# Selective scans in turns: D product to TensorE, positive part and copies to ScalarE, table switches in order

## The chip, the cores and the metric

The kernel runs on one core of one Trainium2 chip. The core has five engines that each work through their own list of instructions in order: TensorE (PE in the profile) multiplies matrices into the accumulators (PSUM), VectorE (DVE) and ScalarE (ACT) work element by element, GpSimd (POOL) does the same more slowly, and SyncE (SP) here only issues DMA transfers. Engines wait for each other by semaphores. The metric is the time of one execution on the device in microseconds (us): median 3931.5, from 3927.8 to 3944.6 over three runs. The execution that was profiled has a span of 3937.4 us.

## The reference

The program is a stack of four layers over an input of 8 images, 128 channels, 16 x 16 pixels: a layer that sums absolute differences to weights, a layer of three selective scans (Mamba) with a small attention, attention with a mixture of experts, and eight Performer layers with a spectral filter. The change touches the scans of the second layer alone. There a sequence of 256 pixels with 256 inner channels is scanned in three orders: forwards (f), backwards (b), and with a stride (s). For each:

```
def mamba_branch(u, cw, cb, xw, dw, db, A_log, D):
    uc = silu(causal_conv1d(u, cw, cb))
    proj = uc @ xw.T                     # dt (8), Bm (16), Cm (16)
    delta = softplus(dt @ dw.T + db)
    return selective_scan(uc, delta, -exp(A_log), Bm, Cm, D)

def selective_scan(u, delta, A, Bm, Cm, D):
    dA = exp(delta[..., None] * A)                       # 16 states
    dBu = (delta * u)[..., None] * Bm[:, :, None, :]
    h = a * h + bu                                       # along the sequence
    y = einsum('lbdn,bln->bld', hs, Cm)                  # sum over the states
    return y + u * D
```

## The kernel before, in words

All data are 32-bit floats. Channels lie on the 128 partitions, in two halves h; the 2048 positions (8 images of 256) are cut into 4 blocks of 512 (two images each). A **unit** is one scan order k and one block t; there are 3 x 4 = 12 units. `_scans` (L429) runs over the units, and for each over its 16 states n (L557 to L585).

One state consists of these instructions, each over both halves (128 x 1024 elements):
- SyncE fetches the rows of B and C for this state, spread over all partitions, from a scratch in DRAM into `bcs` (L560; pool `rows`, four buffers).
- ScalarE forms `da` = exp(delta x A) in two instructions of 128 x 512 (L566), and multiplies the first element of each image by 0, so that images do not run into each other (L569). `da` lies in PSUM, with **two buffers** (`pa`, L442).
- GpSimd forms `dbu` = du x B (L571; two buffers).
- VectorE scans along the sequence, writing the states over `da` (L573), and multiplies by C into `hc` (L577; two buffers). This product is what frees `da` and `bcs`.
- TensorE adds `hc` into the accumulator `acc` by multiplying with the identity (L583, recorded at the helper line L234). `acc` has **one buffer** (`py`, L441), and the sum over 16 states is one accumulation.

When a unit is summed up, `finish` (L533) forms y = uc x D + acc on VectorE, in four pieces of 128 x 256, undoing the scan order in the access patterns (L546). It is called at state 0 of the next unit, behind that state's product.

Beside the states, the next unit is prepared in steps (`prepare`, L471), one step after each state from n = 3 on: GpSimd lays out the input `uo`; TensorE convolves it with diagonal matrices (`taps`, made on GpSimd at L466) into `pc`; ScalarE takes Silu into `uc` (L497); TensorE projects to `pp`, ScalarE copies it to `proj` (L505), and SyncE writes that to DRAM. The softplus follows as max(x, 0) + ln(1 + exp(-|x|)) with a correction of rounding: TensorE forms `pd`; ScalarE |x| (L519); VectorE the positive part into `delta` (L520); ScalarE exp (L521); VectorE r = e + 1 (L523) and the correction e = (r - 1) - e (L524); ScalarE ln r (L525); GpSimd r - e, the sum `delta`, and the product `du` = delta x uc (L527, L528, L531).

Silu needs another function table of ScalarE than exp and ln, and each switch is an instruction of its own.

The order of work: the program text is recorded, and a scheduler then lays down each engine's list by its own estimates of when an instruction is ready. Text order is therefore not the order on an engine. In the order of before, VectorE's list has the scans of two states, then the two products, for 88 pairs of states, and scan and product by turns for 16 states, most of them in the first unit. ScalarE's list also lets exp and Silu change places with each other. Only one kind of instruction is held to the text's order, by `keep_in_program_order` in `ln_exp` (L229), which asks for the table with exp and ln.

Of the kernel before, what the change touches and what calls it, by code (L numbers as in the profile page):

```python
# [10 lines left out]
F32 = mybir.dt.float32  # L11
AF = mybir.ActivationFunctionType
ALU = mybir.AluOpType
# [3 lines left out]
P = 128  # L17
B = 8
L = 256
NT = B * L  # L20
BLK = 512
# [4 lines left out]
NST = 16  # L26
DTR = 8
NPROJ = DTR + 2 * NST
BRANCHES = ("f", "b", "s")
# [148 lines left out]
class Env:  # L178


    def __init__(self, ctx, tc, dram, cols):
        self.tc, self.nc, self.dram = tc, tc.nc, dram
        self.cols = cols
        nc = self.nc
        pool = ctx.enter_context(tc.tile_pool(name="shared", bufs=1))
        self.pool = pool
        self.cst = pool.tile([P, dram["cst"].shape[1]], F32, tag="cst", name="cst")
        self.vecs = pool.tile([P, dram["vecs"].shape[1]], F32, tag="vecs", name="vecs")
        self.rows = pool.tile([P, dram["rows"].shape[1]], F32, tag="rows", name="rows")
        self.mean = pool.tile([P, P], F32, tag="mean", name="mean")  # L190
        self.ones = pool.tile([P, P], F32, tag="ones", name="ones")
        self.eps = pool.tile([P, 1], F32, tag="eps", name="eps")
        nc.gpsimd.memset(self.mean, 1.0 / P)
        nc.gpsimd.memset(self.ones, 1.0)
        nc.gpsimd.memset(self.eps, 1e-5)
        self.X = pool.tile([P, NT], F32, tag="X", name="X")

        self.w = {
            k: pool.tile(list(dram[k].shape), F32, tag="w_" + k, name="w_" + k)
            for k in ("in_proj", "xproj", "dtproj", "out_proj", "qkv", "router", "expert_b", "tok", "enc", "dec")  # L200
        }
# [27 lines left out]
    def ln_exp(self):  # L229

        self.tc.keep_in_program_order(self.nc.scalar.preload_act_table_set("natural_log_exp_and_others"))

    def mm(self, out, lhsT, rhs, start=True, stop=True):
        self.nc.tensor.matmul(out, lhsT=lhsT, rhs=rhs, start=start, stop=stop)  # L234


def bc(ap, axis, n):

    a = ap.unsqueeze(axis)
    shape = list(a.shape)  # L240
    shape[axis] = n
    return a.to_broadcast(shape)
# [30 lines left out]
def blk(i):  # L273
    return slice(i * BLK, (i + 1) * BLK)
# [154 lines left out]
def _scans(E, ctx, xn, y, w_in, w_x, w_dt):  # L429
# [6 lines left out]
    nc, tc = E.nc, E.tc  # L436
    one = ctx.enter_context(tc.tile_pool(name="l1one", bufs=1))
# [6 lines left out]
    ident = E.c("ident")  # L444
# [19 lines left out]
    for k, s in enumerate(BRANCHES):  # L464
        for j in range(8):
            nc.gpsimd.tensor_scalar_mul(taps[:, k, j, :], ident, E.v("cw" + s, j))  # L466

    class Unit:
        pass

    def prepare(U, k, t):  # L471

        s = BRANCHES[k]
        U.k, U.t = k, t

        uo = two.tile([P, 2, 2, L + 3], F32, tag="uo", name="uo")
        nc.gpsimd.memset(uo[:, :, :, 0:3], 0.0)  # L477
        for h in range(2):
            src = u[:, h, blk(t)].rearrange("p (b l) -> p b l", l=L)
            dst = uo[:, h, :, 3:]  # L480
            if s == "f":
                nc.gpsimd.tensor_copy(dst, src)
            elif s == "b":
                nc.gpsimd.tensor_copy(dst, src[:, :, ::-1])
            else:
                for b in range(2):
                    nc.gpsimd.tensor_copy(
                        dst[:, b, :].rearrange("p (i s) -> p i s", s=4),
                        src[:, b, :].rearrange("p (s i) -> p i s", s=4),
                    )  # L490
        yield
        U.uc = uc = two.tile([P, 2, BLK], F32, tag="uc", name="uc")
        for h in range(2):
            pc = ps.tile([P, 2, L], F32, tag="s", name="pc")
            for j in range(4):
                E.mm(pc, taps[:, k, 4 * h + j, :], uo[:, h, :, j : j + L], start=j == 0, stop=j == 3)
            nc.scalar.activation(  # L497
                uc[:, h, :], pc.rearrange("p b l -> p (b l)"), AF.Silu, bias=E.v("cb" + s, h)
            )
        yield  # L500
        proj = two.tile([NPROJ, BLK], F32, tag="proj", name="proj")
        pp = ps.tile([NPROJ, BLK], F32, tag="s", name="pp")
        for h in range(2):
            E.mm(pp, w_x[:, k, h, :], uc[:, h, :], start=h == 0, stop=h == 1)
        nc.scalar.copy(proj, pp)  # L505
        U.bc = scratch.tile([NPROJ, BLK], F32, tag="bc", name="bc")
        nc.sync.dma_start(U.bc, proj)
        yield
        E.ln_exp()


        U.delta = delta = two.tile([P, 2, BLK], F32, tag="delta", name="delta")
        e = one.tile([P, 2, BLK], F32, tag="sp_e", name="sp_e")
        r = one.tile([P, 2, BLK], F32, tag="sp_r", name="sp_r")
        for h in range(2):
            pd = ps.tile([P, BLK], F32, tag="s", name="pd")
            E.mm(pd, w_dt[:, k, h * P : (h + 1) * P], proj[0:DTR, :])
            db = E.v("db" + s, h)
            nc.scalar.activation(e[:, h, :], pd, AF.Abs, bias=db)  # L519
            nc.vector.tensor_scalar(delta[:, h, :], pd, db, 0.0, ALU.add, ALU.max)  # L520
        nc.scalar.activation(e, e, AF.Exp, scale=-1.0)  # L521
        yield
        nc.vector.tensor_scalar_add(r, e, 1.0)  # L523
        nc.vector.scalar_tensor_tensor(e, r, -1.0, e, ALU.add, ALU.subtract)  # L524
        nc.scalar.activation(r, r, AF.Ln)  # L525
        yield
        nc.gpsimd.tensor_sub(r, r, e)  # L527
        nc.gpsimd.tensor_add(delta, delta, r)  # L528
        yield
        U.du = du = two.tile([P, 2, BLK], F32, tag="du", name="du")  # L530
        nc.gpsimd.tensor_mul(du, delta, uc)  # L531

    def finish(U):  # L533

        s = BRANCHES[U.k]
        for h in range(2):
            for b in range(2):
                c = slice(b * L, (b + 1) * L)
                dst = y[U.k][:, h, U.t * BLK + b * L : U.t * BLK + (b + 1) * L]
                a0, a1 = U.uc[:, h, c], U.acc[:, h, c]  # L540
                if s == "b":
                    a0, a1 = a0[:, ::-1], a1[:, ::-1]
                elif s == "s":
                    dst = dst.rearrange("p (s i) -> p s i", s=4)
                    a0, a1 = (v.rearrange("p (i s) -> p s i", s=4) for v in (a0, a1))
                nc.vector.scalar_tensor_tensor(dst, a0, E.v("D" + s, h), a1, ALU.mult, ALU.add)  # L546

    units = [(k, t) for k in range(3) for t in range(NBLK)]
    cur, last = Unit(), None
    for _ in prepare(cur, *units[0]):  # L550
        pass
    for i, _ in enumerate(units):
        nxt, steps = None, iter(())
        if i + 1 < len(units):
            nxt = Unit()
            steps = prepare(nxt, *units[i + 1])
        for n in range(NST):  # L557
            bcs = rows.tile([P, 2, BLK], F32, tag="bcs", name="bcs")
            at = cur.bc[DTR + n : DTR + n + 1, :]
            nc.sync.dma_start(  # L560
                bcs, bass.AP(at.tensor, at.offset, [[0, P], [NST * BLK, 2], [1, BLK]])
            )
            da = pa.tile([P, 2, BLK], F32, tag="da", name="da")
            for h in range(2):
                a = neg_a[:, cur.k, h * NST + n : h * NST + n + 1]
                nc.scalar.activation(da[:, h, :], cur.delta[:, h, :], AF.Exp, scale=a)  # L566

            first = da.rearrange("p h (b l) -> p (h b) l", l=L)[:, :, 0:1]
            nc.scalar.mul(first, first, 0.0)  # L569
            db = two.tile([P, 2, BLK], F32, tag="dbu", name="dbu")  # L570
            nc.gpsimd.tensor_tensor(db, cur.du, bc(bcs[:, 0, :], 1, 2), ALU.mult)  # L571
            flat = da.rearrange("p h l -> p (h l)")
            nc.vector.tensor_tensor_scan(  # L573
                flat, flat, db.rearrange("p h l -> p (h l)"), 0.0, ALU.mult, ALU.add
            )
            hc = two.tile([P, 2, BLK], F32, tag="hc", name="hc")
            nc.vector.tensor_tensor(hc, da, bc(bcs[:, 1, :], 1, 2), ALU.mult)  # L577
            if n == 0:
                if last is not None:
                    finish(last)  # L580
                cur.acc = py.tile([P, 2, BLK], F32, tag="y", name="acc")
            for h in range(2):
                E.mm(cur.acc[:, h, :], ident, hc[:, h, :], start=n == 0, stop=n == NST - 1)  # L583
            if n >= 3:
                next(steps, None)  # L585
        for _ in steps:
            pass
        cur, last = nxt, cur
# [841 lines left out]
```

## Time and profile before

| what | us |
|---|---|
| median time of three runs | 3931.5 |
| span of the profiled execution | 3937.4 |
| first layer, up to the first scan | 1254.6 |
| scans, from the first scan to the last D product | 813.5 |
| attention, fusion and what follows, to 2500 us | 431.9 |
| the rest | 1437.0 |

| in the scan stage | busy us | share of 813.5 |
|---|---|---|
| VectorE | 710.8 | 87% |
| TensorE | 560.7 | 69% |
| GpSimd | 536.8 | 66% |
| ScalarE | 370.4 | 46% |

How to read the profile's lines. A group of instructions has its source line, engine, operation, output and inputs by the program's names, the shapes, and the count; then total busy us and the mean ns of one; then the engine's idle us just ahead of these instructions, and what ended most of it. A line of the timeline has the start in us from the span's start, the us it lasts, engine, line, operation, and the count of like instructions that were merged into it; in brackets the idle time ahead of it and what ended that. "PEclk" is the share of full clock that TensorE was granted, "DMA" the mean busy share of the 16 DMA engines.

### The profile page before, as it was taken

What the parts mean: (1) busy time and instruction counts of PE and PEld (TensorE: products, weight loads), DVE (VectorE), ACT (ScalarE), POOL (GpSimd) and SP (SyncE); (2) the same over time, 40 slices, a digit from 0 to 9 for tenths busy, and PEclk for the clock granted to TensorE, in tenths of its full rate; (3) what the DMA queues carried; (4) which work ended last, traced back from release to release, by engine and by line L of the source; (5) the groups of instructions that cost most, each with busy time, mean ns of one, the idle gap of its engine ahead of it and who ended that gap; (6) DMA issues with size and microseconds to landing.
All of it is one profiled execution on the core that took longest, in us unless ns stands there. A gap on an engine that the chain in (4) does not pass through costs nothing. (4 is left out here: it accounts for less than half of the span.)

```text
span 3937.4 us, 38553 instructions
## 1 busy us (share of the span) xinstructions
PE 3352.6 (85%) x15140; PEld 1684.2 (43%) x15140; DVE 2713.6 (69%) x2920; ACT 2179.7 (55%) x2453; POOL 883.5 (22%) x585
## 2 busy tenths in 40 slices
PE   7999999999998666676768967889999999994999
PEld 3333333333332222222225433366666666662676
DVE  7999999999996988888883123456555555654111
ACT  6999999999995454444531131145554555542111
POOL 0000000000004767666651000122222222220000
PEclk9999999999999889888889986899999999996999
DMA  1000000000001444444430000000000000002000
GB/s 36 1 1 1 1 1 1 1 1 1 1 1 50 129 129 123 124 120 129 119 112 24 0 0 28 30 1 12 12 2 11 12 12 2 11 1 86 0 0 11
DMA packets 62722, 131.59 MB, mean 33 GB/s; under 512 B 4178, under 2 KB 10596, under 8 KB 61772
## 3 DMA queue, kind: packets, MB, share of 16 engines
q1 hardware_dynamic: 60044, 126.01, 10.5%
q10 hardware_dynamic: 2496, 3.11, 0.3%
q8 instruction: 119, 1.95, 0.2%
q14 instruction: 63, 0.52, 0.0%
HBM read 127.08 MB, written 2.03 MB: 33 GB/s over the span
## 5 line engine op out<-in xcount | busy, mean ns | idle before, releaser
L403 ACT ACTIVATE d<-sh,w 128x2048 f32<-128x2048 f32 x576 | 1094.8, 1991 | 80.3 <-PE o L234 70.9
L395 DVE SCALAR_TENSOR_TENSOR acc<-sh,w,acc 128x2048 f32<-128x2048 f32 x448 | 1023.4, 2407 | 0.1
L234 PE MATMUL o<-d,sel 128*32 128x512 f32 x4608 | 928.4, 598 | 12.0 <-ACT d L403 12.0
L234 PE MATMUL acc<-hc,cst 128*128 128x512 f32 x768 | 450.4, 737 | 250.3 <-DVE hc L577 226.5
L234 PEld LDWEIGHTS o<-d,sel 128*32 128x32 f32 x4608 | 322.9, 109 | 563.1 <-issue 412.7
L571 POOL TENSOR_TENSOR dbu<-du,bcs 128x1024 f32<-128x1024 f32 x192 | 449.6, 2357 | 236.2 <-DVE da L573 120.3
L573 DVE TENSOR_TENSOR_SCAN da<-da,dbu 128x1024 f32<-128x1024 f32 x192 | 432.2, 2287 | 91.3 <-ACT da L569 72.9
L566 ACT ACTIVATE da<-delta,neg_a 128x512 f32<-128x512 f32 x384 | 257.3, 687 | 385.9 <-DVE hc L577 381.4
L234 PEld LDWEIGHTS acc<-hc,cst 128*128 128x128 f32 x768 | 169.6, 233 | 527.0 <-DVE hc L577 307.9
L234 PE MATMUL o<-acc,sel 128*32 128x512 f32 x1024 | 292.9, 610 | 45.2 <-DVE acc L395 45.2
L477 POOL MEMSET uo<- 128x12 f32 x12 | 1.3, 112 | 1183.5 <-PE o L234 1169.5
L577 DVE TENSOR_TENSOR hc<-da,bcs 128x1024 f32<-128x1024 f32 x192 | 225.1, 1211 | 1.2
L1375 DVE COPY ug<-p 128x256 f32<-128x256 f32 (+1 forms) x96 | 49.3, 514 | 232.0 <-PE p L234 232.0
L988 DVE SCALAR_TENSOR_TENSOR k<-pq,bias,cst 128x512 f32<-128x512 f32 x64 | 45.1, 747 | 195.6 <-PE pq L234 195.6
L1373 ACT COPY ug<-p 128x256 f32<-128x256 f32 (+1 forms) x96 | 42.6, 444 | 239.2 <-PE p L234 239.2
L234 PE MATMUL p<-T,ut 128*128 128x256 f32 x768 | 172.0, 383 | 0.0
L234 PE MATMUL pq<-u,we 128*128 128x512 f32 x256 | 129.6, 612 | 46.2 <-DVE k L988 46.2
L393 DVE TENSOR_SCALAR acc<-sh,w 128x2048 f32<-128x2048 f32 x128 | 162.7, 1342 | 6.4 <-POOL sh L345 6.4
L234 PEld LDWEIGHTS o<-acc,sel 128*32 128x32 f32 x1024 | 66.2, 111 | 219.1 <-issue 146.9
L234 PEld LDWEIGHTS p<-T,ut 128*128 128x128 f32 x768 | 147.8, 193 | 24.6 <-issue 3.1
L1035 ACT COPY kp<-pf 128x704 f32<-128x704 f32 x64 | 47.8, 746 | 180.1 <-PE pf L234 180.1
L1064 POOL TENSOR_TENSOR kp<-kp,off 128x704 f32<-128x704 f32 x64 | 86.4, 1367 | 209.2 <-DVE off L1050 209.2
(314 smaller groups left out, 4707.4 us busy)
## 6 DMA issues: line engine op xcount, KB each, us to landing
bcs<-bc SPq DMA_DIRECT2D x192, 512.0 KB
m<-in_Mphi SPq DMA_DIRECT2D x4, 2048.0 KB
lw<-in_layers SPq DMA_DIRECT2D x8, 944.0 KB
f<-in_fuse SPq DMA_DIRECT2D x2, 1152.0 KB
T<-in_phi ACTq DMA_DIRECT2D x1, 2048.0 KB
x<-in_x SPq DMA_DIRECT2D x4, 256.0 KB
rows<-in_brow SPq DMA_DIRECT2D x8, 128.0 KB
out_y<-fin SPq DMA_DIRECT2D x4, 256.0 KB
```

Source lines behind the costliest of these rows:

```text
L234: self.nc.tensor.matmul(out, lhsT=lhsT, rhs=rhs, start=start, stop=stop)
L393: nc.vector.tensor_scalar(acc, tap(0), w[:, 0, f : f + 1], None, ALU.max)
L395: nc.vector.scalar_tensor_tensor(acc, tap(k), w[:, k, f : f + 1], acc, ALU.max, ALU.add)
L403: nc.scalar.activation(d, tap(k), AF.Abs, scale=-1.0, bias=w[:, k, f : f + 1])
L566: nc.scalar.activation(da[:, h, :], cur.delta[:, h, :], AF.Exp, scale=a)
L571: nc.gpsimd.tensor_tensor(db, cur.du, bc(bcs[:, 0, :], 1, 2), ALU.mult)
L573: nc.vector.tensor_tensor_scan(flat, flat, db.rearrange("p h l -> p (h l)"), 0.0, ALU.mult, ALU.add)
L577: nc.vector.tensor_tensor(hc, da, bc(bcs[:, 1, :], 1, 2), ALU.mult)
L988: nc.vector.scalar_tensor_tensor(x, pq[:, r, :].rearrange("p (b l) -> p b l", l=L), w["bias"][:, b : b + 1], bc(E.c(table), 1, 2), ALU.add ...
L1035: nc.scalar.copy(kp[:, 2 * b : 2 * b + 2, :], pf[:, :, 0:HM])
L1064: nc.gpsimd.tensor_tensor(kp[:, cs, :].rearrange("p c (h m) -> p c h m", m=M), kp[:, cs, :].rearrange("p c (h m) -> p c h m", m=M), bc(off ...
L1375: nc.vector.tensor_copy(dst, p4)
```

## The change

Four things are done, all inside the scans:
- **Turns.** A new helper, `after(key, ins)`, ties an instruction behind the last one with the same key in the scheduler's graph, without a semaphore. With the key "scan" VectorE's list is held to scan, product, scan, product.
- **Tables.** With the key "tables" the Silu, the explicit switch back to the table of exp and ln, and all Exp and Ln of the scans keep the text's order on ScalarE, so that there is one switch each way per unit.
- **D on TensorE.** Diagonal matrices of D (`dd`) are made once on GpSimd. `acc` starts with dd x uc, and the states are added to it; so `finish` only has to copy `acc` out, which ScalarE does in two pieces of 128 x 512.
- **Softplus.** The positive part becomes a Relu with bias on ScalarE, and r = e + 1 an Identity with bias there. The correction e stays on VectorE.

VectorE is left with scan, product and one correction per unit.

```
+    def after(self, key, ins):
+        last = self.chains.get(key)
+        if last is not None:
+            self.tc.add_manual_dep(
+                ins.ins,
+                last.ins.name,
+                mybir.DependencyInfo(mybir.DependencyClass.NoSync, mybir.DependencyReason.DATA),
+                reason=key,
+            )
+        self.chains[key] = ins
...
+    dd = one.tile([P, 6, P], F32, tag="dd", name="dd")
+    for k, s in enumerate(BRANCHES):
+        for h in range(2):
+            nc.gpsimd.tensor_scalar_mul(dd[:, 2 * k + h, :], ident, E.v("D" + s, h))
...
-            nc.scalar.activation(
-                uc[:, h, :], pc.rearrange("p b l -> p (b l)"), AF.Silu, bias=E.v("cb" + s, h)
+            E.after(
+                "tables",
+                nc.scalar.activation(uc[:, h, :], pc.rearrange("p b l -> p (b l)"), AF.Silu, bias=E.v("cb" + s, h)),
             )
+        E.after("tables", nc.scalar.preload_act_table_set("natural_log_exp_and_others"))
...
-        E.ln_exp()
...
-            nc.vector.tensor_scalar(delta[:, h, :], pd, db, 0.0, ALU.add, ALU.max)
-        nc.scalar.activation(e, e, AF.Exp, scale=-1.0)
+            nc.scalar.activation(delta[:, h, :], pd, AF.Relu, bias=db)
+        E.after("tables", nc.scalar.activation(e, e, AF.Exp, scale=-1.0))
         yield
-        nc.vector.tensor_scalar_add(r, e, 1.0)
+        nc.scalar.activation(r, e, AF.Identity, bias=E.ones[:, 0:1])
         nc.vector.scalar_tensor_tensor(e, r, -1.0, e, ALU.add, ALU.subtract)
-        nc.scalar.activation(r, r, AF.Ln)
+        E.after("tables", nc.scalar.activation(r, r, AF.Ln))
...
-            for b in range(2):
-                c = slice(b * L, (b + 1) * L)
-                dst = y[U.k][:, h, U.t * BLK + b * L : U.t * BLK + (b + 1) * L]
-                a0, a1 = U.uc[:, h, c], U.acc[:, h, c]
...
-                nc.vector.scalar_tensor_tensor(dst, a0, E.v("D" + s, h), a1, ALU.mult, ALU.add)
+            dst = y[U.k][:, h, blk(U.t)].rearrange("p (b l) -> p b l", l=L)
+            a = U.acc[:, h, :].rearrange("p (b l) -> p b l", l=L)
...
+            nc.scalar.copy(dst, a)
...
-                nc.scalar.activation(da[:, h, :], cur.delta[:, h, :], AF.Exp, scale=a)
+                E.after("tables", nc.scalar.activation(da[:, h, :], cur.delta[:, h, :], AF.Exp, scale=a))
...
-            nc.vector.tensor_tensor_scan(
-                flat, flat, db.rearrange("p h l -> p (h l)"), 0.0, ALU.mult, ALU.add
+            E.after(
+                "scan",
+                nc.vector.tensor_tensor_scan(
+                    flat, flat, db.rearrange("p h l -> p (h l)"), 0.0, ALU.mult, ALU.add
+                ),
             )
-            nc.vector.tensor_tensor(hc, da, bc(bcs[:, 1, :], 1, 2), ALU.mult)
+            E.after("scan", nc.vector.tensor_tensor(hc, da, bc(bcs[:, 1, :], 1, 2), ALU.mult))
...
             for h in range(2):
-                E.mm(cur.acc[:, h, :], ident, hc[:, h, :], start=n == 0, stop=n == NST - 1)
+                if n == 0:
+                    E.mm(cur.acc[:, h, :], dd[:, 2 * cur.k + h, :], cur.uc[:, h, :], start=True, stop=False)
+                E.mm(cur.acc[:, h, :], ident, hc[:, h, :], start=False, stop=n == NST - 1)
```

More of the change, by code (lines that the diff above doesn't have):

```diff
@@ L183, in __init__ @@
         self.cols = cols
+        self.chains = {}
         nc = self.nc
@@ L536, in finish @@
         for h in range(2):
-            for b in range(2):
-                c = slice(b * L, (b + 1) * L)
-                dst = y[U.k][:, h, U.t * BLK + b * L : U.t * BLK + (b + 1) * L]
-                a0, a1 = U.uc[:, h, c], U.acc[:, h, c]
[L541 to L546, printed above, removed]
+            dst = y[U.k][:, h, blk(U.t)].rearrange("p (b l) -> p b l", l=L)
+            a = U.acc[:, h, :].rearrange("p (b l) -> p b l", l=L)
+            if s == "b":
+                a = a[:, :, ::-1]
+            elif s == "s":
+                dst = dst.rearrange("p b (s i) -> p b s i", s=4)
+                a = a.rearrange("p b (i s) -> p b s i", s=4)
+            nc.scalar.copy(dst, a)
     units = [(k, t) for k in range(3) for t in range(NBLK)]
```

## The prediction

> **What bounds the kernel now.** I read the page's busy shares first, then the busy time of the scan stage as one stretch, then the groups, and last the order of time on each engine. The change touches only the scans, which run from the first scan at 1254.6 us to the last D product at 2068.1 us:
>
> ```profile
> core 0: us, PE busy (x) PEld busy (x) DVE busy (x) ACT busy (x) POOL busy (x), PEclk, DMA share, GB/s
> 1254.62:2068.09 813.47, 560.73 (x1014) 211.38 (x1012) 710.76 (x476) 370.36 (x677) 536.81 (x259) 0.85 0.42 123
> ```
>
> VectorE (DVE) is busy 711 of 813 us (87%), TensorE 69%, GpSimd (POOL) 66%, ScalarE (ACT) 46%, the DMA engines 42%. So VectorE bounds the stage, yet 103 us of it are idle. The page's groups say what a state costs:
>
> ```profile
> L571 POOL TENSOR_TENSOR dbu<-du,bcs 128x1024 f32<-128x1024 f32 x192 | 449.6, 2357 | 236.2 <-DVE da L573 120.3
> L573 DVE TENSOR_TENSOR_SCAN da<-da,dbu 128x1024 f32<-128x1024 f32 x192 | 432.2, 2287 | 91.3 <-ACT da L569 72.9
> L566 ACT ACTIVATE da<-delta,neg_a 128x512 f32<-128x512 f32 x384 | 257.3, 687 | 385.9 <-DVE hc L577 381.4
> L577 DVE TENSOR_TENSOR hc<-da,bcs 128x1024 f32<-128x1024 f32 x192 | 225.1, 1211 | 1.2
> ```
>
> Nearly all of VectorE's idle time here is ahead of the scan, 72.9 us of it for `da`, while ScalarE itself idles 381 us waiting for the product `hc` (L577), which frees `da`. Each waits for the other over two buffers. The timeline of VectorE shows why. In the first unit states stand in turns, scan, product, scan, product:
>
> ```profile
> 1292.05 2.30 DVE L573 TENSOR_TENSOR_SCAN da<-da,dbu 128x1024 f32<-128x1024 f32 x1 [2.23 <-POOL dbu L571]
> 1294.44 1.23 DVE L577 TENSOR_TENSOR hc<-da,bcs 128x1024 f32<-128x1024 f32 x1
> 1295.59 2.29 DVE L573 TENSOR_TENSOR_SCAN da<-da,dbu 128x1024 f32<-128x1024 f32 x1
> 1297.96 1.23 DVE L577 TENSOR_TENSOR hc<-da,bcs 128x1024 f32<-128x1024 f32 x1
> 1299.11 2.29 DVE L573 TENSOR_TENSOR_SCAN da<-da,dbu 128x1024 f32<-128x1024 f32 x1
> ```
>
> A state takes 1299.11 - 1295.59 = 3.52 us with no gap. In later units two scans stand ahead of two products:
>
> ```profile
> 1371.59 4.48 DVE L573 TENSOR_TENSOR_SCAN da<-da,dbu 128x1024 f32<-128x1024 f32 x2 [1.08 <-ACT da L569]
> 1375.98 2.33 DVE L577 TENSOR_TENSOR hc<-da,bcs 128x1024 f32<-128x1024 f32 x2
> 1379.40 4.48 DVE L573 TENSOR_TENSOR_SCAN da<-da,dbu 128x1024 f32<-128x1024 f32 x2 [1.08 <-ACT da L569]
> 1383.79 2.33 DVE L577 TENSOR_TENSOR hc<-da,bcs 128x1024 f32<-128x1024 f32 x2
> 1388.52 1.66 DVE L546 SCALAR_TENSOR_TENSOR yf<-uc,vecs,acc 128x256 f32<-128x256 f32 x4 [2.40 <-PE acc L234]
> 1390.09 4.47 DVE L573 TENSOR_TENSOR_SCAN da<-da,dbu 128x1024 f32<-128x1024 f32 x2
> ```
>
> Here no `da` is free until the first product of a pair, so the scan waits 1.08 us in each: 1379.40 - 1371.59 = 7.81 us for two states, against 7.04 in turns. The last lines show the end of a unit: VectorE waits 2.40 us for TensorE's last sum and spends 1.66 us on the D product (L546). In the instruction order of before, 88 pairs hold 176 of the 192 states; 16 stand alone.
>
> **What the Trainium skill says.** "ScalarE: Activation LUTs", What ACT_TABLE_LOAD costs, puts a switch of tables at 1283 ns for the load and some 1380 ns more for a drain. The trace agrees on the load (1283 ns) and not on the drain: an activation starts 1.30 us after the load that began at 1321.97. I use 1.28. "SBUF — State Buffer", Who interferes with whom, says that a VectorE instruction with two SBUF inputs, or in a two-port mode, and a GpSimd instruction reading SBUF block each other whole. The trace agrees: the `r` addition (L523) took 0.68 us once and 2.06 us beside `dbu`. That addition leaves VectorE; the subtraction behind it (L524, two SBUF inputs) stays. "Perfetto Trace Analysis", Optimizing Scalar/DVE Operations, allows moving work from a saturated VectorE to ScalarE; at 46% busy ScalarE has room on average, so order within a unit decides.
>
> **The change, part by part.**
>
> *Turns.* 88 pairs x (7.81 - 7.04) = 68 us gone, if nothing else ends the wait. In turns ScalarE has this much room:
>
> ```profile
> 1302.74 1.42 ACT L566 ACTIVATE da<-delta,neg_a 128x512 f32<-128x512 f32 x2 [1.92 <-DVE hc L577]
> 1304.19 0.16 ACT L569 ACTIVATE da<-da 128x4 f32<-128x4 f32 x1
> ```
>
> So `da` is ready 1.72 us after its buffer comes free, and wanted 3.52 us after: 1.8 us of slack per state.
>
> *Off VectorE.* Per unit the D product (1.65 to 2.4 us, plus up to 2.75 of waiting), the positive part (1.40) and the addition (0.7 to 2.1) leave; about 6 us x 11 or 12.
>
> *Onto ScalarE.* Per unit two Relu of 128x512 from PSUM (0.69 each, as Abs at L519), one Identity of 128x1024 (1.06, as L521), two copies of 128x512. Copies from strided PSUM are not in the trace: at least 0.69; at most 1.4 times that (L546 rises from 476 to 655 ns in the strided branch), 0.95. I take 0.8. Table loads fall from 38 to about 26 of 1.28 us.
>
> *Onto TensorE.* 24 products (two 0.5 us passes each), about 2 us a unit beside 48.8 of 68.7 busy: hidden under VectorE. They queue behind the two copies, since `acc` has one buffer: last product of the unit, 2.1 us; copies, to 3.7; four matmuls, to 7.6. The third product of the new unit needs its `hc` back at 9.3 us. It costs nothing.
>
> *New waits.* I follow one unit with these durations, from the end of `hc` of state 2 as time 0, in the instruction order of the changed program:
> - State 4: exponentials to 1.5, load to 2.8, first Silu to 3.5, the small multiplication to 3.7. Its scan was due at 3.52: 0.2 lost. Second Silu and load back run to 5.65.
> - State 5: exponentials to 7.1, the copy of `proj` to 7.6, ready 7.8 where 7.27 was due: 0.6 lost. Product 5 ends at 11.4, product 6 at 14.9.
> - The softplus stands ahead of state 7. TensorE gives `pd` at 10.3 (behind product 4); Abs, Relu, Abs, Relu and Exp end at 14.15; an exponential, then Identity, end at 15.9. VectorE, free at 14.9, holds the subtraction L524 next, with every scan queued behind it: 1.05 lost waiting, 1.2 running. Scan 7 starts at 17.15 rather than 14.9: 2.25.
> - Ln ends at 18.3, state 8 is ready in time at 19.9. GpSimd's order is subtraction, `dbu` 9, addition, product `du`, `dbu` 10, at 2.35 each from 18.3: 30.1. Scan 10 was due at 27.7: 2.4 lost. The first unit of before shows the same sequence and loss (2.23, first line of its timeline above):
>
> ```profile
> 1280.31 2.36 POOL L527 TENSOR_TENSOR sp_r<-sp_r,sp_e 128x1024 f32<-128x1024 f32 x1
> 1282.62 2.35 POOL L571 TENSOR_TENSOR dbu<-du,bcs 128x1024 f32<-128x1024 f32 x1
> 1284.93 2.36 POOL L528 TENSOR_TENSOR delta<-delta,sp_r 128x1024 f32<-128x1024 f32 x1
> 1287.37 2.35 POOL L531 TENSOR_TENSOR du<-delta,uc 128x1024 f32<-128x1024 f32 x1
> 1289.67 7.10 POOL L571 TENSOR_TENSOR dbu<-du,bcs 128x1024 f32<-128x1024 f32 x3
> ```
>
> A unit is then 16 x 3.52 + 0.2 + 0.6 + 2.25 + 2.4 = 61.8 us; the last one, which prepares nothing, 56.3. Before, starts of units lie 67.2, 68.3, 69.3 and 68.7 apart, the last took 62.2.
>
> *Start.* The first unit's softplus has no cover: two Relu, and 1.06 for a 0.69 addition, delay the first scan by some 2.7 us, also counting a 0.6 us copy of `uo` that now precedes `du` on GpSimd. The six diagonal matrices of D (0.6 us each, as `taps`) end before the projections that TensorE must finish first; hidden.
>
> *Sum.* First scan 1257.3, 11 x 61.8 = 680, 56.3, and 4 for the last sum and copies: 1997 against 2068, so 71 us less. The orders before and behind the scans are the same, so I carry their time over: 3931.5 - 71 = 3860.
>
> **The rivals.**
> 1. *The new waits vanish.* If GpSimd and the softplus ran earlier than I follow them, only L524 remains: 57.5 a unit, 47 us more saved, 3813. Against: the loss of 2.23 is already in the trace under this order.
> 2. *New waits replace old ones.* ScalarE keeps a fixed order, so a copy waiting for TensorE, or Relu for `pd`, holds the exponentials; and rows must arrive each 3.52 us rather than 3.9. At 65.5 a unit, 41 of 71 us are lost again: 3901. For: GpSimd waits 114.8 us for `bcs` now. Against: those waits come with pairs, which free rows two at a time; in the first unit's turns GpSimd waits only for scans. A row is asked for at a product's end and its `dbu` falls due 5.8 us later, with 2.4 more to spare; in the pairs a `dbu` that waited for its row began at 1341.2, 4.9 us after the product that freed the row's buffer.
> 3. *Slower.* If ScalarE's held order cost over 6.9 us a unit beyond mine, nothing is left; at 72 a unit, 3972. Against: ScalarE's work per unit is 16 x 1.58 for the states and some 12 for preparation and copies, 37 of 62 us.
>
> **How the numbers follow.** My course 0.78; rival 1 0.07; rival 2 0.12; rival 3 0.03. The predicted time is 3860. The strided copies (0.69 to 0.95) and the collision at L524 (up to 2.35 us more a unit, 26 in all) and a better overlap on GpSimd (2.4 less, 26) span 3834 to 3886; runs of before differ by 17 us; I widen to 3830 to 3892, halfway to either rival. Rival 2 at its worst falls within 0.5% of before, so: faster 0.94, same 0.03, slower 0.03.
>
> **What would show it.** Scans and products strictly in turns, `da` waits ahead of the scan down from 72.9 us to some 20; no `delta` or `y` on VectorE; per unit one wait near 1 us at L524 and one near 2.4 us for `dbu`; units 62 us apart, scan stage near 742 us. I am wrong if a wait for `bcs` or the copies shows ahead of scans in most states, if units lie over 65 us apart, or if a later stage moves by more than 10 us.

## The result and the profile after

| | us |
|---|---|
| before, median of 4 executions beside it | 3934.6 (3927.8 to 3944.6) |
| after, median of 4 executions | 3876.7 (3868.5 to 3889.0) |
| after / before | 0.9853 [0.9819, 0.9888] |
| after measured again, median of 6 | 3870.0 (3862.8 to 3877.4) |
| after again / before beside it | 0.9823 [0.9793, 0.9854] |

The forecast was 3860. The busy time of the scan stage of after, from the first scan to 2002.00 us, half a microsecond before the last copy of the last sum ends (columns as for before):

```profile
core 0: us, PE busy (x) PEld busy (x) DVE busy (x) ACT busy (x) POOL busy (x), PEclk, DMA share, GB/s
1257.59:2002.00 744.41, 534.24 (x1062) 190.64 (x1062) 684.52 (x395) 407.23 (x726) 539.19 (x257) 0.96 0.55 134
```

The stage is 69 us shorter than 813.47. VectorE is busy 684.5 us of 744.4 (92%, 87% before) and has 60 us idle instead of 103. The groups of after's page that answer to those of before:

```profile
L587 POOL TENSOR_TENSOR dbu<-du,bcs 128x1024 f32<-128x1024 f32 x192 | 451.2, 2353 | 171.5 <-DVE da L591 169.7
L591 DVE TENSOR_TENSOR_SCAN da<-da,dbu 128x1024 f32<-128x1024 f32 x192 | 439.7, 2290 | 49.1 <-POOL dbu L587 37.7
L582 ACT ACTIVATE da<-delta,neg_a 128x512 f32<-128x512 f32 x384 | 265.4, 691 | 296.0 <-DVE hc L596 285.1
L596 DVE TENSOR_TENSOR hc<-da,bcs 128x1024 f32<-128x1024 f32 x192 | 235.2, 1225 | 18.3 <-issue 1.3
```

The idle time ahead of the scan fell from 91.3 to 49.1 us, and what ends it has changed: 37.7 us are now for `dbu` from GpSimd; for `da`, which took 72.9 before, the list of waits has 10.4. Of the 37.7, 11.7 are the wait for the very first scan, which lies ahead of the stage; the other 26 are eleven waits of 2.36. The 18.3 us ahead of the product (L596) are 0.1 us between each scan and its own product; they are part of the 3.52 us of a state in turns. The timeline of VectorE shows what stands in the way of a unit of pure turns:

```profile
1276.30 2.30 DVE L591 TENSOR_TENSOR_SCAN da<-da,dbu 128x1024 f32<-128x1024 f32 x1 [0.94 <-ACT da L585]
...
1282.21 1.23 DVE L596 TENSOR_TENSOR hc<-da,bcs 128x1024 f32<-128x1024 f32 x1
1283.57 2.07 DVE L542 SCALAR_TENSOR_TENSOR sp_e<-sp_r,sp_e 128x1024 f32<-128x1024 f32 x1
1285.56 2.28 DVE L591 TENSOR_TENSOR_SCAN da<-da,dbu 128x1024 f32<-128x1024 f32 x1
...
1298.56 2.30 DVE L591 TENSOR_TENSOR_SCAN da<-da,dbu 128x1024 f32<-128x1024 f32 x1 [2.36 <-POOL dbu L587]
```

Three losses stand in each of the eleven units that prepare another, always at the same states: about 1 us where the Silus hold up `da` (state 5), 2.2 us at the correction L542 (ahead of state 7), 2.4 us for `dbu` (state 10). GpSimd's timeline over the same stretch shows where the last two come from:

```profile
1282.20 2.36 POOL L587 TENSOR_TENSOR dbu<-du,bcs 128x1024 f32<-128x1024 f32 x1 [1.16 <-DVE da L591]
1286.81 2.36 POOL L545 TENSOR_TENSOR sp_r<-sp_r,sp_e 128x1024 f32<-128x1024 f32 x1 [2.25 <-ACT sp_r L543]
1289.12 2.36 POOL L587 TENSOR_TENSOR dbu<-du,bcs 128x1024 f32<-128x1024 f32 x1
1291.43 2.36 POOL L546 TENSOR_TENSOR delta<-delta,sp_r 128x1024 f32<-128x1024 f32 x1
1293.87 2.35 POOL L549 TENSOR_TENSOR du<-delta,uc 128x1024 f32<-128x1024 f32 x1
1296.18 4.64 POOL L587 TENSOR_TENSOR dbu<-du,bcs 128x1024 f32<-128x1024 f32 x2
```

Sum and product of the softplus (L546, L549) stand back to back ahead of the `dbu` that the scan of 1298.56 waits for: 1296.18 + 2.35 = 1298.5. And the correction starts at 1283.57 while the `dbu` of 1282.20 runs to 1284.56; it ends 1.08 us after that. Alone it takes 1.21 us, beside `dbu` 2.07. The Trainium skill, "SBUF — State Buffer", Who interferes with whom, says that a VectorE instruction with two SBUF inputs and a GpSimd instruction that reads SBUF shut each other out, whoever issues first going on to its end; these starts and ends agree.

Then the stages. "Scans" ends here with the last product `hc`; "fusion" is the rest of the second layer, its small attention included; "behind" is everything from the start of the third layer to the end, and the expert layer is counted from its first expert product to the weights of the next layer:

| profile | first scan | scans | fusion | behind | of it the expert layer |
|---|---|---|---|---|---|
| before | 1254.6 | 809.0 | 209.0 | 1664.8 | 71.8 |
| after | 1257.6 | 741.7 | 207.7 | 1680.2 | 96.0 |
| after, again | 1256.1 | 741.9 | 206.8 | 1665.6 | 66.7 |

The scans of after repeat within 0.2 us, those of before within 1.3 (experiment 7). The work behind them took 15 us longer in the first profile of after, and no longer in the second, with the same program.

### The profile page after: what moved, and what is told of

It reads as the page before. It is cut to its first block, busy times and chain, and to the rows that moved or that the text cites. A ratio compares the mean times of both kernels' runs of the same rounds, so it can differ in the third digit from the quotient of the medians.

```text
span 3887.2 us, 38606 instructions
## 1 busy us (share of the span) xinstructions
PE 3342.9 (86%) x15188; PEld 1665.6 (43%) x15188; DVE 2685.0 (69%) x2836; ACT 2213.5 (57%) x2500; POOL 890.9 (23%) x591
## 5 line engine op out<-in xcount | busy, mean ns | idle before, releaser
L247 PE MATMUL acc<-hc,cst 128*128 128x512 f32 x768 | 406.1, 653 | 204.1 <-DVE hc L596 204.1
L591 DVE TENSOR_TENSOR_SCAN da<-da,dbu 128x1024 f32<-128x1024 f32 x192 | 439.7, 2290 | 49.1 <-POOL dbu L587 37.7
L582 ACT ACTIVATE da<-delta,neg_a 128x512 f32<-128x512 f32 x384 | 265.4, 691 | 296.0 <-DVE hc L596 285.1
L247 PEld LDWEIGHTS acc<-hc,cst 128*128 128x128 f32 x768 | 139.7, 200 | 462.7 <-DVE hc L596 357.2
L596 DVE TENSOR_TENSOR hc<-da,bcs 128x1024 f32<-128x1024 f32 x192 | 235.2, 1225 | 18.3 <-issue 1.3
```

Of the source, the lines that this page charges most:

```text
L582: E.after("tables", nc.scalar.activation(da[:, h, :], cur.delta[:, h, :], AF.Exp, scale=a))
L591: nc.vector.tensor_tensor_scan(flat, flat, db.rearrange("p h l -> p (h l)"), 0.0, ALU.mult, ALU.add),
L596: E.after("scan", nc.vector.tensor_tensor(hc, da, bc(bcs[:, 1, :], 1, 2), ALU.mult))
```

## The experiments

In what follows "scans" is the stage length of this table. Ratios are to the kernel before, run on the same chip beside each.

**1. The turns alone.** The kernel before, with only this added:

```
+            E.after("scan", nc.vector.tensor_tensor_scan(...))
+            E.after("scan", nc.vector.tensor_tensor(hc, da, bc(bcs[:, 1, :], 1, 2), ALU.mult))
```

> The kernel before, with scan and product tied in turns and nothing else changed. Theory 1 (turns carry about half of the gain, the moved work the other half): VectorE keeps about 6 us of positive part, addition, correction and D product per unit, so a unit takes 16 x 3.52 + 6 + the GpSimd wait of 2.4 = 64 to 66 us against 68.7; the scan stage shrinks by 30 to 55 us from 813, the time is 3880 to 3905. Rival (turns are all of it): the scan stage is as in the changed kernel, 744 us, a gain of some 69. Rival (turns are nothing without the moves, because the waits for the last sum and the ScalarE table switches fill the gaps again): within 15 us of before.

Measured: 3898.2 us, 0.9887 [0.9853, 0.9921]; scans 757.5, which is 51.5 less than before, as theory 1 had it, and 15.8 more than after. VectorE is as busy as before (710.8 against 708.3 us): the whole gain is idle time, 100.7 to 46.7 us. Added first, the order of two kinds of instruction gives three quarters of the change's gain in the stage (51.5 of 67.3). The parts do not simply add up: taken out of the whole change, the same order costs more than the whole gain (experiment 2).

**2. The moves without the turns.** The kernel after, with two scans held ahead of two products in all 96 pairs of states (`product()` holds the product `hc`, `finish` and the sums):

```
+            held.append(product)
+            if n % 2:
+                for go in held:
+                    go()
+                held.clear()
```

> The changed kernel, with all its moves, but VectorE's list tied in pairs, two scans and then two products, through all 96 pairs. Theory 1: each pair waits for a free buffer again, 7.81 us or more against 7.04; a unit takes 62.5 plus 2 for the correction and up to 4 for the table switch, 64.5 to 68 us against 62.2; scan stage 775 to 820 against 744; 30 to 75 us slower than the changed kernel. Rival (the moves alone carry the gain): within 10 us of the changed kernel.

Measured: 3949.6 us, 1.0022 [1.0004, 1.0039]; scans 822.6, 80.9 more than after and more than either theory gave. From the waits of this kernel (total us, times, longest):

```profile
POOL dbu L588 <- DMA bcs<-bc: 191.7, 62, 4.5
DVE da L592 <- ACT da L586: 139.4, 91, 4.2
```

A pair waits 139.4/91 = 1.53 us for `da` on average, not 1.08, and GpSimd's waits for `bcs`, 114.8 us before, have grown to 191.7. VectorE is 48 us less busy than before (660.4 against 708.3, by the profile) and the stage is 14 us longer. Relieving the busiest engine was worth nothing as long as a wait for two buffers set the pace. The 14 us cannot all be laid to the moves: this kernel has 8 pairs more than before, some 6 us by an estimate from the 0.77 us that a pair of before lost against turns, and ScalarE's held order besides.

**3. The D product back on VectorE.** The kernel after, with `finish` and the first sum as before:

```
-            nc.scalar.copy(dst, a)
+                nc.vector.scalar_tensor_tensor(dst, a0, E.v("D" + s, h), a1, ALU.mult, ALU.add)
...
-                    E.mm(cur.acc[:, h, :], dd[:, 2 * cur.k + h, :], cur.uc[:, h, :], start=True, stop=False)
```

> The changed kernel with the D product and the copy out of the accumulator back on VectorE as before (four pieces, behind the first product of the next unit), and no dd product on TensorE. Theory: in turns TensorE has finished by then, so VectorE does not wait, and the move is worth its busy time alone, 1.65 us a unit in orders f and b and 2.4 in s: scan stage 742 + 20 to 25. Rival 1: the wait for the last sum of up to 2.75 us comes back too, + 45. Rival 2: the time falls into waits that are there anyway, under 5.

Measured: 3914.7 us, 0.9935 [0.9914, 0.9957]; scans 760.2, 18.5 more than after, a little under the theory's 20 to 25. VectorE is 19.4 us busier; its waits for `dbu` and `da` are the same 37.7 and 10.4 us. In turns the product has its sum at hand: but for the very last unit (2.1 us) VectorE does not wait for it, where the pairs of before showed 2.40. So this part is worth its busy time on VectorE and nothing else.

**4. Positive part and r = e + 1 back on VectorE.**

```
-            nc.scalar.activation(delta[:, h, :], pd, AF.Relu, bias=db)
+            nc.vector.tensor_scalar(delta[:, h, :], pd, db, 0.0, ALU.add, ALU.max)
...
-        nc.scalar.activation(r, e, AF.Identity, bias=E.ones[:, 0:1])
+        nc.vector.tensor_scalar_add(r, e, 1.0)
```

> The changed kernel with the positive part and r = e + 1 back on VectorE. Theory: VectorE gets 1.4 and 0.7 to 2.1 us a unit more, but the chain on ScalarE ahead of the correction gets 2.4 us shorter, so the wait there goes and the move is worth nothing: scan stage within 10 us of 742. Rival: the busy time comes on top, + 23 to 38.

Measured: 3920.2 us, 0.9946 [0.9930, 0.9963]; scans 775.5, 33.8 more than after: my theory fell. The amount lies in the rival's range, but busy time is only part of it: VectorE is 20.9 us busier (705.4 against 684.5) and idles 12.9 us more. ScalarE's waits in this kernel:

```profile
ACT da L582 <- DVE hc L596: 266.3, 135, 5.5
ACT sp_r L543 <- DVE sp_e L542: 88.0, 11, 8.0
```

The logarithm L543 waits 8.0 us a unit for the correction (15.0 us in all in after, 1.4 a unit). It stands in the held order of ScalarE's tables, so the exponentials behind it wait too; VectorE's wait for `da` rises from 10.4 to 45.3 us, while that for `dbu` falls from 37.7 to 19.4. Experiment 1 lays the wait for `da` to the order held on ScalarE and not to the place of the three instructions. There they are on VectorE too, and the D product besides, but ScalarE's order is free:

```profile
DVE da L588 <- ACT da L582: 9.8, 11, 0.9
ACT sp_r L538 <- DVE sp_e L537: 18.9, 11, 1.7
```

Its stage is 18.0 us shorter than here (757.5), with more work on VectorE. Where the D product stands does not bear on this wait: experiment 3 has 10.4 as after does.

**5. ScalarE's order left to the scheduler.** The key "tables" taken from Silu, Exp and Ln, and `ln_exp` put back:

```
-                E.after("tables", nc.scalar.activation(da[:, h, :], cur.delta[:, h, :], AF.Exp, scale=a))
+                nc.scalar.activation(da[:, h, :], cur.delta[:, h, :], AF.Exp, scale=a)
```

> The changed kernel without the order of tables on ScalarE (the former request for the table of exp and ln in its old place). The built order then has 77 table loads in the scans instead of some 24, about 53 x 1.28 = 68 us more on ScalarE. Theory: many are alone in a state and fit into the 1.8 us of room there, but those next to a Silu or the softplus come on top: scan stage + 10 to 40. Rival: ScalarE has room on average (55% busy), so under 5.

Measured: 3881.6 us, 0.9858 [0.9824, 0.9893]; scans 733.5, 8.2 less than after. The trace shows 71 table loads in the stage instead of 22, some 63 us more on ScalarE at 1.28 each, and they did not lengthen the stage; that theory fell. The scheduler parts the two Silus and puts the correction where GpSimd mostly is not reading (mean 1.40 us, 2.07 in after). VectorE waits 30.0 us for `da` and 27.0 for `dbu`, together no less than in after; it is 9.4 us less busy (675.1 against 684.5), most of it the correction. So the held order of tables, one of the four parts of the change, did not pay in the stage. The time as a whole is not below that of after (0.9858 against 0.9853 and 0.9823); the one profile here has the longer time behind the scans (experiment 7).

**6. The change once more.**

> The changed kernel once more, for a second profile. Theory A (the loss of 27 us in the expert layer, where TensorE ran at half its clock, belongs to that one execution): the scan stage is again 744 us within 2, and the expert layer, from its first bias product to the weights of the next layer, takes near 75 us as before rather than 101. Theory B (the denser scans cause it): the expert layer takes some 100 us again.

Its numbers are in the section on the result. Theory A holds: 741.9 for the scans (744 counts to the last copy), 66.7 instead of 96.0 for the expert layer (72.1 instead of 101.4 if counted from the first bias product, as the expectation does). In the first profile of after, over three stretches of 10 us of that layer:

```profile
2375.00:2385.00 10.00, 10.00 (x12) 3.17 (x11) 2.45 (x4) 0.00 (x0) 0.00 (x0) 0.50 0.00 0
2385.00:2395.00 10.00, 10.00 (x12) 3.02 (x11) 1.68 (x3) 0.00 (x0) 0.00 (x0) 0.50 0.00 0
2395.00:2405.00 10.00, 10.00 (x15) 3.21 (x14) 2.75 (x4) 0.00 (x0) 0.00 (x0) 0.67 0.00 0
```

and the same stretches of the second:

```profile
2375.00:2385.00 10.00, 10.00 (x22) 3.43 (x22) 3.76 (x6) 0.00 (x0) 0.00 (x0) 1.00 0.00 0
2385.00:2395.00 10.00, 10.00 (x23) 3.29 (x21) 3.79 (x6) 0.00 (x0) 0.00 (x0) 1.00 0.00 0
2395.00:2405.00 10.00, 10.00 (x21) 3.71 (x21) 4.12 (x6) 0.00 (x0) 0.00 (x0) 0.92 0.00 0
```

The layer starts at 2369.7 in both. TensorE is busy throughout; in one execution it is granted half its clock (third column from the right) for over 25 us, in the other it has the full clock within 5. In both it had begun to work 9 us before the layer, at half its clock, after the same idle time (6.63 and 6.64 us). So neither the work nor the gap ahead of it tells the two apart.

**7. The kernel before once more**, to see whether it too takes the longer way behind the scans.

> The kernel before once more, with a profile. Theory A (the stages behind the scans take one of two times in any kernel, whatever its scans do): the scan stage takes 809 within 3 us, and the stages from the attention on take either about 1665 us, as in the first profile, or about 1678, as in most profiles of the kernel after. Theory B (the moves of the change made the later stages slower): always about 1665 here. One more profile at 1678 settles it for A; one at 1665 leaves it where it is.

Measured: 3937.5 us, 1.0002 [0.9988, 1.0016]; scans 807.7, behind 1661.5. That leaves the matter where it was for before. Over all fourteen profiles of this study the part behind the scans falls into two groups of seven, 1659 to 1666 us and 1676 to 1682. They are the groups of the expert layer too: 67 to 72 us in the seven short ones, 88 to 96 in the seven long ones. Both profiles of before lie in the lower, but so do the second of after and those of experiments 2, 9 and 10, which contain every move of work of the change (experiment 2 without its turns). So the moves do not force the longer time; whether they make it more frequent is open.

**8. Spreading GpSimd's work, first try.** The kernel after, with the softplus on GpSimd tied between the `dbu` of states 8, 9 and 11, and two more ScalarE instructions held in order:

```
-        nc.scalar.copy(proj, pp)
+        E.after("tables", nc.scalar.copy(proj, pp))
...
+        E.after("pool", nc.gpsimd.tensor_sub(r, r, e))
+        yield
+        E.after("pool", nc.gpsimd.tensor_add(delta, delta, r))
...
+            E.after("pool", nc.gpsimd.tensor_tensor(db, cur.du, bc(bcs[:, 0, :], 1, 2), ALU.mult))
```

> The changed kernel, with GpSimd's three softplus instructions spread over four states and tied in that order among the dbu, and the small multiplication and the copy of proj tied in order on ScalarE, so that the Silu no longer stands between an exponential and its scan. Theory (the waits that I followed in the unit are single, and vanish when their cause is moved): the 2.36 us wait for dbu goes from each of 11 units, 26 us, and of 1.1 us at the Silu some 0.7 remain at most; the scan stage is 705 to 720 against 744. Rival (the waits only move on, since GpSimd's work per unit has to be done somewhere): less than 10 us.

Measured: 3874.2 us, 0.9838 [0.9796, 0.9879]; scans 737.3, 4.4 less than after: a miss, and the rival's case. The wait for `dbu` did fall, 37.7 to 21.6, but that for `da` rose from 10.4 to 23.2: the copy of `proj`, now held in place, waits 3 us a unit for TensorE (32.6 us in all) with the exponentials behind it. The two ties on ScalarE were not tried one by one; experiment 11 has the small multiplication tied and the copy free, and a wait for `da` of 10.2.

**9. Only GpSimd's list ordered.** The ties on ScalarE taken out again, and the layout of `uo` moved two units ahead, behind state 5.

> The changed kernel, where GpSimd's list alone is held to an order: its three softplus instructions at states 8, 9 and 11, and the layout of uo at state 5, for the unit after the next. ScalarE's list is left as in the changed kernel. Theory (each of GpSimd's extra 2.35 us fits into the 1.17 us of idle time of two states, if they do not stand together): the 2.36 us wait for dbu goes from every unit and nothing comes in its place, scan stage 742 - 26 = 716. Rival (as in the first try at this, the wait moves on): 730 or more.

Measured: 3849.4 us, 0.9776 [0.9750, 0.9801]; scans 718.8. On another occasion:

> The kernel with only GpSimd's order changed, once more on this chip for comparison: scan stage 719 within 3 us; the stages behind it either some 1665 or some 1678 us; time 3845 to 3865.

3843.3 us, 0.9755 [0.9732, 0.9778]; scans 718.8, and these waits on VectorE:

```profile
DVE da L600 <- POOL dbu L596: 14.4, 5, 10.8
DVE da L600 <- ACT da L594: 10.4, 11, 0.9
```

Of the 14.4, 10.8 are the first scan. The eleven waits of 2.36 have shrunk to 3.6 us in all, and the stage by 22.9: this loss of after was GpSimd's order.

**10. The softplus in pieces.** Besides, each Silu with its own table switch in states 3 and 4, the softplus one piece per state, and the correction between scan and product:

```
+        E.after("scan", nc.vector.scalar_tensor_tensor(e, r, -1.0, e, ALU.add, ALU.subtract))
+        yield
+        E.after("tables", nc.scalar.activation(r, r, AF.Ln))
+        E.after("pool", nc.gpsimd.tensor_sub(r, r, e))
```

> The spread kernel of before, with one Silu and its own table switch in each of states 3 and 4, the small multiplication tied in ScalarE's order, and the softplus cut into one piece per state, the correction on VectorE between the scan and the product of state 9, so that GpSimd makes no B u beside it. Theory: with no other wait left in a unit the correction costs 1.2 us instead of 2.07 and the wait for da at the Silus goes, so that a unit takes about 57.6 us and the scan stage 690 to 703 us (718.8 before); time about 3825. Rival: the waits move on to operations that ScalarE's held order now puts behind a matmul of TensorE, and the stage stays at 715 or more.

Measured: 3875.6 us, 0.9848 [0.9817, 0.9879]; scans 743.5, 25 more than experiment 9. The correction did take 1.21 us as meant, but VectorE waited 43.8 us for `dbu`. GpSimd's timeline:

```profile
1546.25 2.35 POOL L553 TENSOR_TENSOR sp_r<-sp_r,sp_e 128x1024 f32<-128x1024 f32 x1 [3.37 <-ACT sp_r L552]
1548.55 2.35 POOL L599 TENSOR_TENSOR dbu<-du,bcs 128x1024 f32<-128x1024 f32 x1
1550.86 2.35 POOL L555 TENSOR_TENSOR delta<-delta,sp_r 128x1024 f32<-128x1024 f32 x1
1553.17 2.34 POOL L599 TENSOR_TENSOR dbu<-du,bcs 128x1024 f32<-128x1024 f32 x1
1555.48 2.34 POOL L558 TENSOR_TENSOR du<-delta,uc 128x1024 f32<-128x1024 f32 x1
```

It idles 3.37 us for the logarithm with a `dbu` that could have run behind it, and then has 2.35 + 2.35 = 4.7 us of work in each of three states, where a state lasts 3.52.

**11. The same pieces, two states apart.** The Silus in states 2 and 4; GpSimd's three operations behind the `dbu` of states 12, 13 and 15.

> The previous kernel with the same pieces moved apart: the two Silus in states 2 and 4, GpSimd's subtraction behind B u of state 12 (the logarithm has then long ended), its addition behind 13, du behind 15, and the layout of uo tied behind B u of state 5 in every branch. Theory: an operation of 2.35 us on GpSimd costs nothing if it has two states to itself, since B u leaves 1.17 us free in each; the correction, on VectorE between scan and product, is then the only loss, 1.2 us; a unit takes 57.6 us and the scan stage 690 to 703 us, time about 3825. Rival: what was lost by the piecewise kernel lay in cutting up ScalarE's work, not in GpSimd's order; then it stays above 715.

Measured: 3836.7 us, 0.9726 [0.9696, 0.9755]; scans 698.5, as the theory had it; faster than both kernels. VectorE's waits in the stage, of which 10.8 are the first scan:

```profile
DVE da L608 <- POOL dbu L604: 10.8, 1, 10.8
...
DVE da L608 <- ACT da L602: 10.2, 11, 1.0
```

and the correction in place:

```profile
1527.61 2.29 DVE L608 TENSOR_TENSOR_SCAN da<-da,dbu 128x1024 f32<-128x1024 f32 x1
1529.81 1.21 DVE L553 SCALAR_TENSOR_TENSOR sp_e<-sp_r,sp_e 128x1024 f32<-128x1024 f32 x1
1530.93 1.21 DVE L615 TENSOR_TENSOR hc<-da,bcs 128x1024 f32<-128x1024 f32 x1
```

The `dbu` just behind it takes 3.25 us instead of 2.35: the correction now issues first, GpSimd is the one held up, and it has the time.

```profile
1529.98 3.25 POOL L604 TENSOR_TENSOR dbu<-du,bcs 128x1024 f32<-128x1024 f32 x1 [1.17 <-DVE da L608]
```

192 states at 3.52 are 676 us; 11 corrections 13 and 11 waits of about 1 us for `da` make 699. The profiled execution has the longer time behind the scans.

## Why the prediction came out as it did

The direction and the mechanism were right, the time 17 us too low in the first set of runs and 10 in the second. Step by step:

- **Turns**, 68 us: right in kind, and by far the largest part. Alone they gave 51.5, since new waits for GpSimd come with them: that for `dbu` is 34.2 us there and was 18.2 before (10.8 of each the start). This 16.0 is nearly all that is missing from the 68. That turns would do most of it could be read in before: its first unit, with all but one pair in turns, took 62.1 us from first scan to first scan, as long as a unit of after, though the softplus of the next unit was still on VectorE (the D product of a unit falls into the unit behind it).
- **New waits**, 5.45 us a unit: measured in the first unit 0.2 (state 4), 1.0 (state 5, 0.6 foretold), 2.2 (softplus) and 2.4 (`dbu`), together 5.8, at the states that were foretold; units lie 62.2 us apart (1338.52 to 1400.72) for a forecast of 61.8. The 2.25 for the softplus is right only in sum. I had 1.05 of waiting and 1.2 of running; it is 0.2 of waiting and 2.0 of running, because I left the collision with `dbu` to the range, though I had the 2.06 us of the addition in front of me. That the two errors cancel is luck. The waiting is short because Identity ends 0.5 us sooner than I followed it (the four Abs and Relu start 0.57 us apart, not 0.69) and VectorE comes 0.4 later. At state 5 I had left out that the copy of `proj` itself waits 0.61 us for TensorE.
- **Off VectorE**, about 6 us a unit: too high as a saving of its own. On top of the turns the moves gave 24.0 us in the stage, 2 a unit, where ScalarE's order stayed free (757.5 in experiment 1, 733.5 in experiment 5), and 15.8 with the held order of the change. The D product is worth 18.5 us in the stage, all of it busy time; the 2.75 us of waiting belonged to the pairs and had gone with them.
- **Onto ScalarE**: a copy from PSUM takes 0.59 us in all three orders (0.8 taken, 0.69 to 0.95 allowed: the lower end, taken from a function with a bias, was no lower bound for a plain copy). Identity takes 1.16 (1.06). Table loads fell to the 26 that were forecast (22 of them in the stage, 32 before). The Trainium skill, "ScalarE: Activation LUTs", What ACT_TABLE_LOAD costs, gives a price per load; that it was not worth saving here is experiment 5.
- **Onto TensorE**, nothing: right. Its products fit. Its granted clock in the stage rose from 0.85 to 0.96, and it was busy 534 us instead of 561 with more products; the prediction did not foresee this.
- **Start**, 2.7 us: 3.0 between the first profiles, but 0.4 between the second ones (1255.7 and 1256.1). With the same program the first scan moves by 1.1 us (before) and 1.5 us (after) from one profile to the next, so the hit is in part luck.
- **Sum**: the last copy ends at 2002.5 where 1997 was forecast, 65.6 us earlier than before, not 71. The eleven units took 685 us where 680 were due, and that is the difference.
- **"The orders before and behind the scans are the same, so I carry their time over"**: this step failed in the first profile. The order is the same, the time was 15 us longer: the expert layer took 24 us more, with TensorE at half its clock for a part of it (experiment 6), and the rest behind the scans 9 us less. It is the case that the prediction named against itself, a later stage that moves by more than 10 us. Of the shortfall in the profiles (3887.2 where 3937.4 - 71 = 3866.4 was due, 20.8 us) 15 lie there and 5 in the scans. In the second profile, where the time behind the scans is that of before, 3870.4 stand against 3866.4. The sum of the change's own stage was nearly right, and what stood outside it was taken as fixed.
- **Rival 1** (the waits vanish, 57.5 a unit) did not come, but its price was nearly right: experiment 11 reaches 58.4 a unit ((698.5 - 56.3)/11), and 3836.7 us where the rival had 3813. **Rival 2** did not come in the change; experiments 4 and 8 show that its mechanism, ScalarE's held order, is real.
- **Slips in the sums**, none of which moves the 3860: the gain of 71 us is used up at 6.5 us a unit, not at 6.9; 3830 and 3892 do not lie halfway to 3813 and 3901 (that would be 3836 and 3880); 3901 lies 0.8% below before, not within 0.5%. The unit lengths of before run from one D product to the next, so that the first, 67.2, holds 17 states and the last, 62.2, holds 15. From first scan to first scan they are 62.1, 64.9, and then 67 to 70 us, and the last takes 65.5.

## What to carry to other kernels

Where two engines hand two buffers back and forth, look at the order on the engine that frees them before moving work off it: here the turns alone gained 51.5 us, the moves with the pairs kept gained nothing (a stage 14 us longer), and on top of the turns they were worth 24.0, of which the held order of ScalarE took 8.2 away again. Whether a third buffer would have done what the turns do was not tried. In such a loop every engine has a budget per turn (here 3.52 us; GpSimd uses 2.35 and has 1.17 to spare). Extra work of 2.35 us cost nothing here where it had two turns to itself (experiment 11), and held the loop up where it came three turns running (experiment 10). Hold in order only what must be: an instruction that waits for another engine, tied ahead of the loop's own, stops the loop.

## What the runs showed of the hardware that was not expected

- TensorE's granted clock can stay at one half for over 25 us while it is busy 100%: groups of four matmuls take 3.78 us instead of 1.98, so it is more than an entry in the clock record. The Trainium skill, "TensorE: Matmul & The Clock Gate", What's actually happening, has activity release the throttle. The second profile of after agrees in kind: the full clock came some 12 us after TensorE began to work. The first does not: it took 35. The section Seeing it yourself there warns of stretches stuck at a low clock (at a quarter there, one half here). What decides between the two courses no run here shows.
- Which of VectorE and GpSimd is held up depends on which issues first, and 0.17 us ahead is enough: correction first, 1.21 and 3.25 us (experiment 11); `dbu` first, 2.07 and 2.36 (after).
- Undoing PSUM's scan order by a reversed or a strided access pattern costs ScalarE's copy nothing: 589, 588 and 588 ns in the median for the three orders.
